# Products of halves one block earlier, weight additions on Pool, and finer steps in a retention and FFN kernel

## The chip, the cores and the metric

The kernel runs on one core of a Trainium2 chip. The metric is device time in microseconds, the median of several runs of one program. The kernel before had 993.59 us (992.89 to 993.91 in 3 runs).

## The reference

All is float32. x has 4 sequences of 1024 tokens and 512 features, here 4096 rows.

```
xn  = layernorm(x)
q, v = xn @ Wq.T, xn @ Wv.T                 # 16 heads of 32
ret[t] = lam * ret[t-1] + v[t]              # per sequence and head
y   = layernorm(q * ret) * silu(xn @ Wg.T)
x1  = x + layernorm(y @ Wo.T)
n   = layernorm(x1)                         # weights below rounded to float8 e4m3
h   = silu(n @ gate_w * gate_s) * (n @ up_w * up_s)      # 512 -> 1536
out = x1 + layernorm(h @ down_w * down_s)
```

## The kernel before, in words

The rows are cut into 8 blocks of 512 tokens, numbered 0 to 7. For each block there is an attention part (class `Retention`: xn, v with its scan, q, y, g, the output projection o and x1) and an FFN part (class `Ffn`: gate, up, fuse, down). Block 0's attention stands alone at the start. Then the loop at L973 runs over t = 0 to 7; in each turn the FFN of block t, in 12 iterations i (128 of the 1536 inner features each), is woven together with the attention of block t+1 (`b`), the preparation of block t+2 (`n`: statistics, xn, its transpose by way of DRAM) and the end of the FFN of block t-1 (`l`: scale, statistics, residual).

Every instruction goes through `InOrder` (L66): an engine executes its instructions in the order in which the program text emits them. Nothing overtakes on an engine's queue, nor on the queues from which SP issues DMAs. Engines wait for one another by semaphores that the tile framework places.

TensorE's work for a block is: v, q and g, 4 projections each of 4 float32 matmuls of 512 columns (L282); o, 4 more; a mean and a variance over features by a matmul with a constant matrix, whose input is split into a rounded upper half and a rest (`halves`, L575); and the FFN, in which gate, up and down are each 8 matmuls of a cheaper type (fp32r), 4 for the upper half of x1n and 4 for its rest.

From block FAST on (L330, 3 before) v, q and g are computed from 7 products of halves instead of 8: the 512 by 512 weight is cut into four quarters, and so is the input; `order` (L333) lists the products, `product` (L461) does one, 4 matmuls of 256 columns, and adds it up with the others on DVE. Four of the seven need sums of weight quarters (5, 6, 7 and 3 in `weight_sums`, L339); these were made on DVE in the first two iterations of t = 1 and stored to DRAM. The weights of the products are fetched into a ring of 4 buffers by SP (`fetch_weights`, L364), which takes the place of the square weights in SBUF. Four of the seven need differences of input quarters (`input_sums`, L445), which Pool computes into `t_sums` from the transposed xn. Products 1, 6 and 2 of v are done in the last iteration of the turn before.

Three other things lie around the change:

- Rounding of the FFN weights to float8 values (`round_weights`, L183) goes on piece by piece during block 0's attention and the first 8 iterations of t = 0: for each piece an integer mask on DVE (the "unit"), two activations on ACT, an addition and a subtraction on DVE, 1024 elements a row, and then the load of a further piece on SP. `rounds(3)` does one piece.
- A search for weights that overflow (`find_over`, L228) runs over the FFN weights on ACT in t = 1 in 24 activations, spread by the list `look`; `pass_over` (L247) adds up what it found in t = 2 with a matmul, and puts it into the down scale.
- PSUM has 2 banks for attention (`pa0`, `pa1`), 2 for gate and up (`pf`), 4 for down.

Of the kernel before, what the change touches and what calls it, by code (L numbers as in the profile page):

```python
# [10 lines left out]
F32 = mybir.dt.float32  # L11
# [4 lines left out]
ALU = mybir.AluOpType  # L16

P = 128
# [5 lines left out]
def retention_ffn_sandwich(  # L24
# [20 lines left out]
    NT, D = x.shape  # L45
# [20 lines left out]
    class InOrder:  # L66
# [113 lines left out]
    def load_piece(n):  # L180
        sp.dma_start(as_dst(parts[places[n][0]], n), pieces[n][1])
# [64 lines left out]

    def pass_over():  # L247

        dve.reduce_sum(total, over, mybir.AxisListType.X)
        po = ps_tile("over_all")  # L250
        pe.matmul(po[:, :1], mean_w, total, start=True, stop=True)
        dve.tensor_scalar(total, po[:, :1], 3e38, 3e38, ALU.mult, ALU.mult)
        dve.tensor_scalar(total, total, 0.0, None, ALU.mult)
        dve.tensor_scalar(ds_sb, ds_sb, total, None, ALU.add)


    def stats(src, mv):
# [78 lines left out]
    squares = {"v": (wvT, wv_sb), "q": (wqT, wq_sb), "g": (wgT, lambda: wg_sb)}  # L336
    operands = {}

    def weight_sums():  # L339

        for k, (src, w) in squares.items():
            w = w() if callable(w) else w
            v = src.rearrange("(c p) f -> p c f", p=P)
            a11, a12, a21, a22 = (w[:, i : i + 2, o : o + H] for o in (0, H) for i in (0, 2))
            operands[k] = {1: v[:, 0:2, 0:H], 2: v[:, 2:4, 0:H], 4: v[:, 2:4, H:D]}
            done = {}
            for j, x, y, op in (
                (5, a21, a22, ALU.add), (6, 5, a11, ALU.subtract),
                (7, a11, a21, ALU.subtract), (3, a12, 6, ALU.subtract),
            ):  # L350
                t = work.tile([P, D], F32, tag="tok", name=f"sum_{k}{j}", bufs=4)
                done[j] = t.rearrange("p (c f) -> p c f", c=2)
                x, y = (done[o] if isinstance(o, int) else o for o in (x, y))
# [5 lines left out]
    sums = weight_sums()  # L359
    RING = 4  # L360
    total_products = len(order) * (NB - FAST)
    fetched = [0]
# [476 lines left out]
    for n in range(4):  # L839
        load_piece(n)  # L840
    wg_sb = load_square(wgT, "wg_sb")
    a = Retention(0, x_first)
    a.new_xnT()
    warm(14)
# [18 lines left out]
    b = Retention(1)  # L863
# [108 lines left out]
    l = None  # L972
    for t in range(NB):  # L973
        f, n = Ffn(a), None
        fast = b is not None and b.fast
        for i in range(NI):
            if t > 0 and (t > 1 or i):
                (f if i else l).rest((i - 1) % NI)
            if t == 0 and i == 0:
                n = Retention(2)  # L980
# [10 lines left out]
            if l and b and not fast and i == 3:  # L991
                l.norm(0)
                l.add(0)
                l.norm(1)
                l.add(1)
# [8 lines left out]
            if n and i == 6 and t > 0:  # L1004
                n.stats(2)
                n.stats(3)
                n.rstd()
                if n.fast:
                    n.shift()
            if b and not fast and i == 5:  # L1010
                b.z(0)
            if b and i >= 8:
# [21 lines left out]
            if b and not fast and t > 0 and i < 3:  # L1034
                b.v(i + 1)
                b.scan(i + 1)
            if l and b and not fast and i == 2:
                l.stats(0)
                l.stats(1)
            if b and not fast and i == 3:  # L1040
                b.halves()
                units()
                if t == 0:
                    rounds(3, now=False)
                b.g_of(0)
                b.mean()
                b.center_y()
                if t == 0:
                    n.stats(3)
                    n.rstd()  # L1050
                    n.shift()
            if b and not fast and i == 4:
                b.halves()
                if t == 0:
                    rounds(3, now=False)
                b.g_of(1)
                b.var()
            if b and not fast and i == 5:
# [2 lines left out]
            if b and not fast and i == 6:  # L1061
                b.g_of(3)
                b.z(2)
                if t == 0:
                    b.z(3)
            if b and 7 <= i <= 10:
                b.o(i - 7)
            if b and i == 8:
# [14 lines left out]
            if b and not fast and i == 4:  # L1083
                b.rstd_y()
            if n and i == 11:
                if n.fast:
                    n.products(2)
                else:
                    n.v(0)
                    n.scan(0)  # L1090
# [28 lines left out]
            for _ in range((look[i] + 1) // 2 if t == 1 else 0):  # L1119
                next(search)  # L1120

            if l and b and not fast and i == 2:
                l.stats(2)
                l.stats(3)
                l.rstd()
# [5 lines left out]
            if l and b and not fast and i == 3:  # L1131
                l.norm(2)
                l.add(2)
                l.norm(3)
                l.add(3)
            if b and not fast and t > 0 and i < 3:
                b.q(i + 1)
                b.y_of(i + 1)
            if b and not fast and i == 6 and t > 0:
                b.z(3)  # L1140
            if n and i == 5 and t == 1:
                n.stats(0)
                n.stats(1)
            if n and i == 6:
                n.new_xnT()
            if b and 7 <= i <= 10:
# [1 line left out]
            if b and i >= 9:  # L1148
                b.rest_of(i - 9)
            if n and t > 0 and 6 <= i <= 9:  # L1150
                n.norm_x(i - 6, n.fast)
                n.send_x(i - 6)
            if t == 0 and i in (5, 6):
                n.send_x(2 * i - 10)
# [3 lines left out]
            if b and n and i == 11:  # L1158
                b.rest_of(3)
            if n and i == 11:  # L1160
                if n.fast:
                    n.product()
                    n.input_sums(3, 4)
                else:
                    n.q(0)
                    n.y_of(0)

            if i == f.lag:
                f.sums()
# [21 lines left out]
            if n and n.fast and i == 11:  # L1191
                n.product()
            if n and t > 1 and i == 5:
# [19 lines left out]
        l, a, b = f, b, n  # L1213
# [68 lines left out]
```

## Time and profile before

| | before |
|---|---|
| median of 3 runs | 993.59 us |
| the profiled execution | 991.89 us |
| its span, first to last instruction | 990.1 us |
| granted TensorE clock | 0.998 |
| busy PE / DVE / ACT / POOL | 968.6 / 657.1 / 365.3 / 256.4 us |
| one f32 projection, 4 matmuls of 512 columns | 3.43 us |
| one FFN group, 8 fp32r matmuls of 512 columns | 1.83 us |
| block 2's first v matmul to block 3's | 192.27 to 315.39 us |
| one turn with a fast block, from t = 3 on | 118.6 us |

A line of a timeline has the start in us from the span's start, the duration, the engine, the line of the code (here always L74, the recording helper), the operation, out<-in by the program's tile names, the shape, and how many instructions are merged; in brackets the idle time before it and who ended it. A line of waits has who waited for whom, the us in total, how often, and the longest. Names: pv, pq, pg are projections or products of v, q, g; pfg, pfu, pd those of the FFN; po the output projection; mu and var the mean and variance; half a half of their input; mv the layernorm statistics; scr the weights that are rounded; seen the search; xnT the transposed xn.

### The profile page before, as it was taken

Reading aid. Unit: us, or ns where it says so; the run is one execution under the profiler, and the core shown is the slowest. Engines: PE = TensorE matmul, PEld = TensorE weight load, DVE = VectorE, ACT = ScalarE, POOL = GpSimd, SP = SyncE. Lnnn points to the kernel's source line nnn. Section 1 sums busy time; section 2 is a strip of 40 time slices with the busy share of each in tenths; the row PEclk is TensorE's granted clock in tenths of the full one; section 3 lists DMA queues with packets and bytes.
Section 4 is the critical chain, followed back from the end, with each engine's and each line's share of the span. In section 5 each row is a group of like instructions: output and inputs, shape, how many; then the busy total and the mean of one; then the engine's idle time right before and its main releaser. Section 6 shows DMA issues by size and latency. Waiting matters only on the chain.

```text
span 990.1 us, 11037 instructions
## 1 busy us (share of the span) xinstructions
PE 968.6 (98%) x3878; PEld 722.0 (73%) x3878; DVE 657.1 (66%) x1006; ACT 365.3 (37%) x549; POOL 256.4 (26%) x337
## 2 busy tenths in 40 slices
PE   9999999999999999999999999999999999999996
PEld 7455766666666878678876788767887788877885
DVE  5996978548746567665686566866567656756445
ACT  3556575433765125221432114321152211512223
POOL 1405121203314033240513305132141312322020
PEclk9999999999999999999999999999999999999999
DMA  9312314412136326253243633245241542213021
GB/s 295 119 64 73 119 64 104 130 64 85 65 98 149 126 69 229 80 144 118 85 128 90 160 91 109 94 129 157 76 149 57 136 138 75 75 32 117 0 86 43
DMA packets 85223, 104.56 MB, mean 106 GB/s; under 512 B 7728, under 2 KB 49712, under 8 KB 85168
## 3 DMA queue, kind: packets, MB, share of 16 engines
q1 hardware_dynamic: 83584, 102.92, 34.5%
q10 hardware_dynamic: 1584, 0.94, 0.5%
q8 instruction: 31, 0.51, 0.2%
q14 instruction: 24, 0.20, 0.1%
HBM read 71.06 MB, written 32.77 MB: 105 GB/s over the span
## 4 chain that ended last, share of the span: by engine, by line
PE 86%; DVE 6%; POOL 3%; ACT 2%; issue 1%; DMA 1%; ACTq 0%; DVEq 0%; SPq 0%; POOLq 0%
PE pfu L74 16%; PE pfg L74 16%; PE pd L74 15%; PE pv L74 10%; PE pg L74 10%; PE pq L74 9%; PE po L74 9%; POOL t_sums L74 1%; DVE st L74 1%; DVE fuse L74 1%; POOL mv L74 1%; DVE scr L74 1%; ACT seen L74 1%; POOL x L74 1%; DVE d L74 1%
## 5 line engine op out<-in xcount | busy, mean ns | idle before, releaser
L74 PE MATMUL pfu<-x1nT,up_sb 128*128 128x512 f32 x768 | 212.1, 418 | 0.0
L74 PE MATMUL pfg<-x1nT,gate_sb 128*128 128x512 f32 x768 | 194.3, 395 | 0.4 <-DVE x1nT L74 0.4
L74 PE MATMUL pd<-down_sb,fuse 128*128 128x512 f32 x720 | 187.2, 401 | 0.0
L74 PEld LDWEIGHTS pfu<-x1nT,up_sb 128*128 128x128 f32 x768 | 144.5, 188 | 44.4 <-issue 14.4
L74 PEld LDWEIGHTS pfg<-x1nT,gate_sb 128*128 128x128 f32 x768 | 144.1, 188 | 30.4 <-DVE x1nT L74 0.8
L74 PEld LDWEIGHTS pd<-down_sb,fuse 128*128 128x128 f32 x720 | 135.3, 188 | 29.3 <-issue 1.7
L74 ACT CAST fuse<-gate 128x512 fp32r<-128x512 f32 x90 | 55.7, 618 | 236.4 <-DVE gate L74 236.4
L74 ACT ACTIVATE gate<-pfg,gs_sb 128x512 f32<-128x512 f32 x96 | 65.7, 684 | 206.2 <-PE pfg L74 206.1
L74 DVE SCALAR_TENSOR_TENSOR gate<-pfu,us_sb,gate 128x512 f32<-128x512 f32 x96 | 71.6, 746 | 82.8 <-PE pfu L74 82.8
L74 PE MATMUL po<-wo_sb,y 128*128 128x512 f32 x256 | 114.5, 592 | 0.0
L74 POOL TENSOR_SCALAR mv<-mv 128x1 f32<-128x1 f32 (+1 forms) x82 | 18.6, 226 | 302.6 <-DVE mv L74 301.6
L74 PEld LDWEIGHTS po<-wo_sb,y 128*128 128x128 f32 x256 | 48.2, 189 | 50.3 <-issue 46.9
L74 DVE TENSOR_TENSOR fuse<-gate,fuse 128x512 fp32r<-128x512 f32 x90 | 75.6, 840 | 9.1 <-ACT fuse L74 9.1
L74 POOL TENSOR_TENSOR ysum<-y 128x256 f32<-128x256 f32 (+1 forms) x13 | 13.5, 1038 | 188.8 <-DVE y L74 161.1
L74 POOL TENSOR_TENSOR x<-x,x1n 128x512 f32<-128x512 f32 x32 | 46.7, 1460 | 45.7 <-DVE x1n L74 36.7
L74 DVE BATCH_NORM_STATS2 st<-x 128x6 f32<-128x512 f32 x64 | 43.6, 681 | 13.7 <-POOL x L74 11.2
L74 DVE TENSOR_TENSOR mids<-pv,mids 128x512 f32<-128x512 f32 x25 | 17.3, 691 | 46.3 <-PE pv L74 43.4
L74 POOL TENSOR_TENSOR mv<-mv,nhalf 128x1 f32<-128x1 f32 (+1 forms) x75 | 45.3, 604 | 6.2
L74 PE MATMUL pv<-xnT,wv_sb 128*128 128x512 f32 (+1 forms) x120 | 42.9, 508 | 1.6 <-ACT xnT L74 1.6
L74 PE MATMUL pv<-t_sums,w_ring 128*128 128x256 f32 x160 | 38.3, 382 | 5.6 <-POOL t_sums L74 5.6
L74 PE MATMUL pq<-xnT,wq_sb 128*128 128x512 f32 (+1 forms) x112 | 43.4, 531 | 0.0
L74 PE MATMUL pg<-xnT,wg_sb 128*128 128x512 f32 x96 | 43.0, 592 | 0.0
(156 smaller groups left out, 1334.5 us busy)
## 6 DMA issues: line engine op xcount, KB each, us to landing
kept<-x SPq DMA_DIRECT2D x32, 256.0 KB, 2.1
x<-kept SPq DMA_DIRECT2D x32, 256.0 KB, 3.7
x<-in_x SPq DMA_DIRECT2D x28, 256.0 KB, 4.1
out<-d SPq DMA_DIRECT2D x27, 256.0 KB, 2.0
xnT<-mx SPq DMA_DIRECT2D x24, 256.0 KB, 4.8
mxs<-xs SPq DMA_DIRECT2D x84, 64.0 KB, 1.8
x1n<-mxs SPq DMA_DIRECT2D x21, 256.0 KB, 2.7
mx<-xn SPq DMA_DIRECT2D x20, 256.0 KB, 2.3
```

Of the source, the lines that this page charges most:

```text
L74: return lambda *args, **kwargs: tc.keep_in_program_order(op(*args, **kwargs))
```

## The change

- FAST is 2: block 2, too, goes by products of halves. Block 1 is the last that goes the old way, so the branches for slow blocks in later turns fall away.
- The weights' sums are made on Pool, in iterations 0 to 2 of t = 0 (v, then q, then g, 4 additions each), into 4 buffers used in turn; SP stores them at the end of the same iteration. The ring of weights is set up at the end of iteration 7 of t = 0, not of iteration 6 of t = 1.
- The first of Pool's four input additions is emitted at the end of iteration 10, not in iteration 11; the second stays in iteration 11.
- The search's last step is a generator in three parts: the sum at the end of iteration 0 of t = 2, the matmul in iteration 1 before the up product, the rest behind the gate step of iteration 1. It was all at the end of iteration 1.

```diff
     def pass_over():
         dve.reduce_sum(total, over, mybir.AxisListType.X)
+        yield
         po = ps_tile("over_all")
         pe.matmul(po[:, :1], mean_w, total, start=True, stop=True)
+        yield
         dve.tensor_scalar(total, po[:, :1], 3e38, 3e38, ALU.mult, ALU.mult)
         dve.tensor_scalar(total, total, 0.0, None, ALU.mult)
         dve.tensor_scalar(ds_sb, ds_sb, total, None, ALU.add)
+        yield
...
-    FAST = 3
+    FAST = 2
...
-                dve.tensor_tensor(done[j], x, y, op)
-                operands[k][j] = dram.tile([P, 2, H], F32, tag=f"sum_{k}{j}", name=f"dsum_{k}{j}", bufs=1)
-                sp.dma_start(operands[k][j], done[j])
-                yield
+            pool.tensor_tensor(done[j], x, y, op)
+        return done
+
+    def keep_sums(k, done):
+        for j, t in done.items():
+            operands[k][j] = dram.tile([P, 2, H], F32, tag=f"sum_{k}{j}", name=f"dsum_{k}{j}", bufs=1)
+            sp.dma_start(operands[k][j], t)
...
+            if t == 2 and i == 1:
+                next(passing)
...
+            if t == 0 and i < 3:
+                k = "vqg"[i]
+                done = weight_sums(k)
...
-            if n and n.fast and i == 11:
-                n.input_sums(1, 2)
+            if n and i == 11:
+                n.input_sums(2)
             units()
             f.up(i)
             f.fuse(i)
...
+            if t == 2 and i == 1:
+                next(passing)
             if fast and i < 6:
                 b.product()
...
+            if n and i == 10:
+                n.input_sums(1)
+            if n and i == 11:
                 n.product()
+            if t == 0 and i < 3:
+                keep_sums(k, done)
...
-            if t == 1 and i < 2:
-                for _ in range(6):
-                    next(sums, None)
-            if t == 1 and i == 6:
+            if t == 0 and i == 7:
                 t_sums = wpool.tile([P, 4, 2, H], F32, tag="wv_sb", name="t_sums")
...
-            if t == 2 and i == 1:
-                pass_over()
+            if t == 2 and i == 0:
+                next(passing)
```

More of the change, by code (lines that the diff above doesn't have):

```diff
@@ L254, in pass_over @@
         dve.tensor_scalar(ds_sb, ds_sb, total, None, ALU.add)
+        yield
+    passing = pass_over()
     def stats(src, mv):
@@ L335, in retention_ffn_sandwich, with weight_sums @@
     banks = {"v": {1: 0, 6: 1, 5: 0}, "q": {1: 1, 6: 0, 5: 1}, "g": {1: 0, 6: 0, 5: 1}}
-    squares = {"v": (wvT, wv_sb), "q": (wqT, wq_sb), "g": (wgT, lambda: wg_sb)}
+    squares = {"v": (wvT, wv_sb), "q": (wqT, wq_sb)}
     operands = {}
[L339 to L353, printed above, removed]
-                dve.tensor_tensor(done[j], x, y, op)
-                operands[k][j] = dram.tile([P, 2, H], F32, tag=f"sum_{k}{j}", name=f"dsum_{k}{j}", bufs=1)
-                sp.dma_start(operands[k][j], done[j])
-                yield
-    sums = weight_sums()
+    def weight_sums(k):
+        src, w = squares[k]
+        v = src.rearrange("(c p) f -> p c f", p=P)
+        a11, a12, a21, a22 = (w[:, i : i + 2, o : o + H] for o in (0, H) for i in (0, 2))
+        operands[k] = {1: v[:, 0:2, 0:H], 2: v[:, 2:4, 0:H], 4: v[:, 2:4, H:D]}
+        done = {}
+        for j, x, y, op in (
+            (5, a21, a22, ALU.add), (6, 5, a11, ALU.subtract),
+            (7, a11, a21, ALU.subtract), (3, a12, 6, ALU.subtract),
+        ):
+            t = work.tile([P, D], F32, tag="tok", name=f"sum_{k}{j}", bufs=4)
+            done[j] = t.rearrange("p (c f) -> p c f", c=2)
+            x, y = (done[o] if isinstance(o, int) else o for o in (x, y))
+            pool.tensor_tensor(done[j], x, y, op)
[4 more added lines that the diff above has]
+            sp.dma_start(operands[k][j], t)
     RING = 4
@@ L841, in retention_ffn_sandwich @@
     wg_sb = load_square(wgT, "wg_sb")
+    squares["g"] = wgT, wg_sb
     a = Retention(0, x_first)
@@ L990, in retention_ffn_sandwich @@
                     l.scale(s)
[L991 to L995, printed above, removed]
             if l and not b and i in (6, 7):
@@ L1007, in retention_ffn_sandwich @@
                 n.rstd()
-                if n.fast:
-                    n.shift()
+                n.shift()
             if b and not fast and i == 5:
@@ L1033, in retention_ffn_sandwich @@
                 b.y_of(i + 2)
[L1034 to L1039, printed above, removed]
+            if t == 0 and i < 3:
+                k = "vqg"[i]
+                done = weight_sums(k)
             if b and not fast and i == 3:
@@ L1042, in retention_ffn_sandwich @@
                 units()
-                if t == 0:
-                    rounds(3, now=False)
+                rounds(3, now=False)
                 b.g_of(0)
@@ L1047, in retention_ffn_sandwich @@
                 b.center_y()
[L1048 to L1051, printed above, removed]
+                n.stats(3)
+                n.rstd()
+                n.shift()
             if b and not fast and i == 4:
                 b.halves()
-                if t == 0:
-                    rounds(3, now=False)
+                rounds(3, now=False)
                 b.g_of(1)
@@ L1063, in retention_ffn_sandwich @@
                 b.z(2)
-                if t == 0:
-                    b.z(3)
+                b.z(3)
             if b and 7 <= i <= 10:
@@ L1082, in retention_ffn_sandwich @@
             f.fuse(i)
-            if b and not fast and i == 4:
+            if t == 0 and i == 4:
                 b.rstd_y()
             if n and i == 11:
[L1086 to L1090, printed above, removed]
+                n.products(2)
                 b.turn_x1n(3, "pf")
                 b.upper_of(3)
+            if t == 2 and i == 1:
+                next(passing)
             if fast and i < 6:
@@ L1120, in retention_ffn_sandwich @@
                 next(search)
[L1122 to L1125, printed above, removed]
             if l and not b and i in (4, 5):
@@ L1130, in retention_ffn_sandwich @@
                     l.rstd()
[L1131 to L1143, printed above, removed]
             if n and i == 6:
@@ L1150, in retention_ffn_sandwich @@
             if n and t > 0 and 6 <= i <= 9:
-                n.norm_x(i - 6, n.fast)
+                n.norm_x(i - 6, True)
                 n.send_x(i - 6)
@@ L1160, in retention_ffn_sandwich @@
             if n and i == 11:
[L1161 to L1166, printed above, removed]
+                n.product()
+                n.input_sums(3, 4)
             if i == f.lag:
@@ L1190, in retention_ffn_sandwich @@
                 b.rstd_y()
-            if n and n.fast and i == 11:
+            if n and i == 10:
+                n.input_sums(1)
+            if n and i == 11:
                 n.product()
-            if n and t > 1 and i == 5:
+            if t == 0 and i < 3:
+                keep_sums(k, done)
+            if n and t > 0 and i == 5:
                 n.stats(0)
                 n.stats(1)
-            if t == 1 and i < 2:
-                for _ in range(6):
-                    next(sums, None)
-            if t == 1 and i == 6:
+            if t == 0 and i == 7:
                 t_sums = wpool.tile([P, 4, 2, H], F32, tag="wv_sb", name="t_sums")
```

## The prediction

> **What bounds the kernel now.** The page first: the TensorE matmul row is busy for 98% of the span, and the chain that ended last is 86% PE.
>
> ```profile
> span 990.1 us, 11037 instructions
> PE 968.6 (98%) x3878; PEld 722.0 (73%) x3878; DVE 657.1 (66%) x1006; ACT 365.3 (37%) x549; POOL 256.4 (26%) x337
> PE 86%; DVE 6%; POOL 3%; ACT 2%; issue 1%; DMA 1%; ACTq 0%; DVEq 0%; SPq 0%; POOLq 0%
> ```
>
> So an edit counts for what it takes from PE's row, and for each moment at which PE must stand still. Next, the waits of PE, all that there are above 0.9 us:
>
> ```profile
> PE pv L74 <- POOL t_sums L74: 5.6, 5, 1.1
> PE pv L74 <- ACT xnT L74: 1.6, 2, 1.2
> PE var L74 <- ACT half L74: 1.4, 1, 1.4
> PE pv L74 <- DMA mxs<-xs: 1.3, 1, 1.3
> PE idle L74 <- DVE nhalf L74: 1.0, 1, 1.0
> PE over_all L74 <- DVE total L74: 1.0, 1, 1.0
> ```
>
> Three of them are the change's: t_sums (x's additions, once per fast block), over_all (the search's last step), and the DMA, which is block 3's x arriving. Last, the timeline of DVE where PE leaves block 0's third up product and comes to block 1's mean:
>
> ```profile
> 117.54 0.68 DVE L74 TENSOR_TENSOR fuse<-gate,fuse 128x512 fp32r<-128x512 f32 x1
> 118.14 0.68 DVE L74 BATCH_NORM_STATS2 st<-x 128x6 f32<-128x512 f32 x1
> 118.86 0.18 DVE L74 BATCH_NORM_AGGREGATE mv<-st 128x2 f32<-128x6 f32 x1
> 118.96 0.66 DVE L74 TENSOR_TENSOR half<-ysum,half 128x512 fp32r<-128x512 f32 x1
> ```
>
> The second half of the mean's matmul needs that "half", which ends at 119.62; PE's mean is at 118.83 to 120.01. DVE has no idle time from 108.81 to there. In this place DVE, not PE, sets the pace, with nothing to spare.
>
> **What the Trainium skill says.** GPSIMD Engine Reference, 1. Specifications: Pool's SBUF interfaces are shared with VectorE, and it collides with DVE instructions that have two SBUF inputs or run in a two-port mode. VectorE: DVE Perf Modes, The perf-mode tier table: a float32 tensor_tensor runs at 1x, a tensor_scalar from SBUF at 2x, an operand in PSUM excludes the two-port mode. The trace agrees on both. Its timelines of DVE and of Pool in block 0's attention:
>
> ```profile
> 45.30 1.98 DVE L74 TENSOR_TENSOR scr<-scr 128x1024 f32<-128x1024 f32 x1
> 47.31 2.18 DVE L74 TENSOR_TENSOR gate_sb<-scr 128x1024 fp32r<-128x1024 f32 x1
> 49.42 1.76 DVE L74 TENSOR_SCALAR scr<-scr 128x1024 int32<-128x1024 int32 x1
> ```
> ```profile
> 44.93 5.70 POOL L74 TENSOR_TENSOR sqsum<-sqsum,sq 128x512 f32<-128x512 f32 x3 [1.29 <-ACT sq L74]
> ```
>
> Alone these take 1.22, 1.22 and 0.68 us on DVE, and 1.26 each on Pool. Here they alternate: each waits for the other's to end, so DVE stood 0.76, 0.96 and 1.08 us, about 1 us for each Pool instruction. Operations with PSUM (gate, y from pq) and bn_stats show no such wait beside a busy Pool. ScalarE activation tables: per-element evaluation and per-set limits, What a function is on this engine: changing between table sets costs 1283 ns; the trace has 1.28 us.
>
> **The change, part by part.** The sum is against the profiled execution: 990.1 us of span and 1.8 around it, 991.89; the median shown is 993.59, 1.7 above, and the difference is put on that.
>
> 1. *Block 2's products.* Twelve projections of 3.43 us (chain, "PE pv L74 x8") become 21 products of about 1.73 (three iterations with three products each, 322.82 to 333.49, are 10.67 us, less six FFN groups of 1.82 make 5.2 per three): 41.2 against 36.4, less 4.8. Checked on whole blocks: block 2's first product to block 3's is 192.27 to 315.39, less its 1.34 wait, 121.8; a fast block 435.63 to 554.22, less its 1.12 wait, 117.5. That says 4.3, which I take. **-4.3** (bounds 4.0 to 5.0).
>
> 2. *The weights' additions on Pool.* Twelve Pool instructions, 1.26 us each, in block 0's first three iterations, behind ysum (101.53 to 102.82). Taking twelve DVE additions out of block 1 (0.68 us each) gains nothing: PE waits for no DVE there. But on Pool they meet DVE's weight rounding, which is saturated. I walk the two engines' orders with the alternation rule, DVE's own durations from its row in the trace and Pool's 1.26 (number = end in us; what has to alternate is in capitals, and each such step starts 0.1 before the other's end):
>
> ```
> Pool YSUM 102.8 | DVE UNIT 103.4 | V5 104.5 | ROUND 105.6 | V6 106.7 | ROUND 107.8
> V7 108.9 | FUSE0 109.5 | V3 110.6 | DVE statistics 110.2, y 110.8, gate1 111.5
> Pool YSUM 112.2 | UNIT 112.8 | Q5 113.9 | ROUND 115.0 | Q6 116.1 | ROUND 117.2
> Q7 118.3 | FUSE1 118.9 | Q3 120.0 | statistics 119.6, gate2 120.3 | G5 121.3
> UNIT 121.9 | G6 123.0 | ROUND 124.1 | G7 125.2 | ROUND 126.3 | G3 127.4
> FUSE2 128.0 | statistics 128.7 | HALF starts 128.7
> ```
>
> Each q and g addition needs its buffer's store landed (issued on SP 0.4 us apart, 2 us to land): in time. Gate1 frees the PSUM bank that PE needs at 110.36, so PE stands 1.2 there; behind it are the down products and all else. "Half" starts at 128.7, not 118.96, and PE's mean is late by 9.7, the 1.2 included. In short: twelve collisions at 0.9, less 1 us of DVE idle used up at 107.8. After it everything at mean, centring and variance follows as before, shifted. **+9.7**. Below: if a third of the collisions fall on DVE's statistics or PSUM work, 7. Above: 1.08 each with no idle used, 12. A gain is excluded, as PE waits for DVE here now already. Stores: SP's weight loads stand behind four stores each, but each load waits for DVE's rounding longer than Pool takes; nothing.
>
> 3. *x's additions sooner.* In steady blocks Pool's two additions run 435.92 to 438.58, and PE, free at 437.36, starts its second product at 438.64. Now the first addition is issued one iteration earlier. But it needs the transposed x: the last of its four loads is issued at 429.0 and lands 5.9 later, 434.9. It ends at 436.2; the statistics' pair for the last x1 tile (0.19 and 0.55, now at 435.13) stands behind it, ends at 436.95, then the second addition, 438.2. Gain about 0.35 a block, not 1.1, four blocks: **-1.4** (0 to -4.5, if the load lands 1 us sooner). Block 3's x lands at 315.2 already late: first addition to 316.5, the pair, second to 318.6 against 318.4: **+0.1**. Block 2 has such a wait for the first time: Pool's add ends at 191.4, addition to 192.7, pair to 193.5, second to 194.8; PE is ready for it at 193.8: **+1.0** (0.5 to 1.1).
>
> 4. *Block 2 fast beside the search.* ACT's 24 search activations (1.57 us each, and 0.19 to read the sum) stay in block 1's FFN, now amid the fast block's ACT work. Most fit: ACT idles 2 to 6 us in front of each gate. One doesn't. In iteration 4 a search step takes a buffer that the variance's matmul reads, so ACT waits for that matmul, then searches 1.57, then loads a table (1.28, hidden under the wait in a steady block), and only then takes the root. On the steady block's clock: root end 502.2 instead of 499.8; reciprocal to 505.6; DVE catches up by two idle gaps of 0.22 and 0.91; the last gated y is 1.15 late. The output projection starts at 516.86 with next to no slack, so PE stands **+1.0** (0 to 3).
>
> 5. *The search's end in parts.* Its 0.96 wait goes. But the matmul now sits in front of the second up product, and its result is read by DVE only behind that product's gate step (0.67), while PE's next half product needs the same bank: PE waits about 1.1 there. Blocks cost 120.16 with the step and 118.60 without; Behind it on PE stands the rest of the iteration. With 0.2 for the matmul that is 1.3 against 1.56: **-0.2** (-1.0 to +0.5).
>
> 6. *Early ring loads.* Four loads of 256 KB enter SP's queue ahead of block 1's transposes at 168. They may delay ACT by 2 us at 178; the next PE need, a PSUM bank at 190.3, is met at 187.4 now. **0** (to +1).
>
> Sum: -4.3 + 9.7 - 1.4 + 0.1 + 1.0 + 1.0 - 0.2 = **+5.9 us**. 991.89 + 5.9 = 997.8 in a profiled execution; 993.59 + 5.9 = 999.5 for the median.
>
> **The rivals.** *The collisions hide* (faster). Mechanism: Pool's twelve additions fit between DVE's rounding instructions instead of alternating with them. It decides once a Pool addition costs DVE under 0.32 us (3.8 of other gain over twelve); at none the time is 989.8. For: the sums depend on one another, so Pool leaves gaps. Against: all three cases at 45 to 51 us alternate, as does the 2.31 us rounding step at 97.22 beside ysum. Chance 0.15. *Half of it* (the same): stores land late, Pool's additions for g slip behind the mean's half, where DVE's idle 2.87 us at 126 takes part of the loss; 4.9 instead of 9.7 gives 994.7. Chance 0.12. *More waits*: on top of the forecast, the search in iterations 5 and 6 or the ring loads cost 3 to 4 us: 1003. Chance 0.08. That the additions sooner do little is in the forecast already.
>
> **How the numbers follow.** Forecast 0.65 (own range 996.5 to 1002.5). A measurement can tell about 0.2%, 2 us, from no change. Faster by more: 0.15; within: 0.12; slower: 0.73. The range of 8 in 10 reaches from the faster case's near side to the case of more waits, 989.5 to 1003.5.
>
> **What would show it.** Right: Pool's twelve sums lie between 102.8 and about 128, its instructions longer than 1.26, DVE's rounding steps stretched to about 2.2; PE waits for DVE "half" at block 1's mean by about 8 us; t_sums waits of about 0.8 remain in the later blocks; a wait of about 1 us for y at block 2's first output projection; a wait of about 1 us after over_all. Wrong: the mean within 3 us of its present place, or t_sums waits gone.

## The result and the profile after

The changed kernel has 1003.19 us (1001.9 to 1003.75, 4 runs), the kernel before 993.24 us (992.22 to 993.91, 4 runs): ratio 1.0099, 95% interval 1.0082 to 1.0117, slower. The forecast was 999.5. A ratio here and below is to executions of the kernel before that were timed along with the run in question, so that equal medians can have slightly different ratios. The profiled execution has 1001.9 us, its span is 1000.1; before it was 991.89 and 990.1, so 10.0 us have to be found. In the lines PE is TensorE, DVE VectorE, ACT ScalarE and POOL GpSimd.

The page of the kernel after, the lines that answer to those of before:

```profile
span 1000.1 us, 11277 instructions
PE 968.1 (97%) x3950; PEld 737.0 (74%) x3950; DVE 662.3 (66%) x1007; ACT 369.9 (37%) x556; POOL 283.9 (28%) x358
PE 74%; DVE 10%; DMA 5%; ACT 4%; POOL 4%; issue 2%; SPq 1%; ACTq 0%; DVEq 0%; POOLq 0%
```

PE is busy for the same time as before (968.6), in a longer span, although block 2's work shrank by some 4 us: part of what remains ran slower, as shown below. The rest of what was added is standing time, and on the chain that ended last PE's share fell from 86% to 74%. Where PE stands, in the waits of the kernel after:

```profile
PE pv L74 <- POOL t_sums L74: 8.9, 6, 2.8
PE mu L74 <- DVE half L74: 5.9, 1, 5.9
...
PE pv L74 <- DMA xnT<-mx: 1.5, 1, 1.5
PE po L74 <- DVE y L74: 1.2, 1, 1.2
PE pfu L74 <- DVE gate L74: 1.1, 1, 1.1
...
PE pq L74 <- DVE total L74: 1.0, 1, 1.0
```

New are mu (5.9), pfu (1.1) and po (1.2), and t_sums grew from 5.6 to 8.9; over_all's 1.0 has become pq's. The wait of 1.4 at the variance is gone only because PE itself comes there later.

The largest part lies where it was forecast. VectorE from block 0's first gate step to block 1's "half", in the timeline of the kernel after (before, "half" started at 118.96):

```profile
103.43 2.29 DVE L74 TENSOR_TENSOR scr<-scr 128x1024 f32<-128x1024 f32 x1
...
107.85 1.78 DVE L74 TENSOR_TENSOR fuse<-gate,fuse 128x512 fp32r<-128x512 f32 x1
109.56 0.68 DVE L74 BATCH_NORM_STATS2 st<-x 128x6 f32<-128x512 f32 x1
...
122.09 2.18 DVE L74 TENSOR_TENSOR down_sb<-scr 128x1024 fp32r<-128x1024 f32 x1
...
126.67 0.93 DVE L74 TENSOR_TENSOR half<-ysum,half 128x512 fp32r<-128x512 f32 x1
```

And GpSimd in the same stretch:

```profile
102.91 1.73 POOL L74 TENSOR_TENSOR sum_v<-wv_sb 128x512 f32<-128x512 f32 x1
104.71 2.14 POOL L74 TENSOR_TENSOR sum_v<-sum_v,wv_sb 128x512 f32<-128x512 f32 x1
...
112.88 2.35 POOL L74 TENSOR_TENSOR sum_q<-wq_sb 128x512 f32<-128x512 f32 x1 [0.49 <-DMA dsum_v<-sum_v]
...
119.10 1.27 POOL L74 TENSOR_TENSOR sum_q<-wq_sb,sum_q 128x512 f32<-128x512 f32 x1
```

The two alternate: four of the six rounding steps of 1.22 take 2.2 or 2.3, the fuse step of 0.68 takes 1.78, and eleven of GpSimd's twelve additions of 1.26 take 1.7 to 2.35. The statistics (0.68) beside them are not stretched, and one addition, at 119.10, took 1.27. "Half" starts 7.7 later than before. PE, first in the kernel before and then in the kernel after:

```profile
120.01 2.00 PE L74 MATMUL pfu<-x1nT,up_sb 128*128 128x512 f32 x8
121.85 1.98 PE L74 MATMUL pd<-down_sb,fuse 128*128 128x512 f32 x8
123.67 1.98 PE L74 MATMUL pfg<-x1nT,gate_sb 128*128 128x512 f32 x8
...
131.51 2.00 PE L74 MATMUL pfu<-x1nT,up_sb 128*128 128x512 f32 x8
```
```profile
127.66 0.80 PE L74 MATMUL mu<-half,mean_r 128*128 128x512 f32 x1 [5.88 <-DVE half L74]
128.25 3.62 PE L74 MATMUL pfu<-x1nT,up_sb 128*128 128x512 f32 x8
131.66 2.80 PE L74 MATMUL pd<-down_sb,fuse 128*128 128x512 f32 x8
134.30 1.98 PE L74 MATMUL pfg<-x1nT,gate_sb 128*128 128x512 f32 x8
...
140.57 2.02 PE L74 MATMUL pfu<-x1nT,up_sb 128*128 128x512 f32 x8
```

The up product behind the mean starts 8.24 later; that is the additions, with 0.1 of a later start. Then the up and down products take 3.62 and 2.80 instead of 2.00 and 1.98, and the gate product is 10.63 late: 2.4 us go without any wait. The granted TensorE clock was 0.57 from 127.66 to 134.30; in the kernel before it was 1.00 from 120.01 to 123.67. Of the 10.63, 1.57 come back, since PE no longer waits at the variance, and PE's first product behind the variance moves from 131.51 to 140.57: 9.06 in all. Followed along PE: 9.35 at block 2's first product (192.11, now 201.46), 9.39 at block 3's first (315.39, now 324.78), 9.78 at block 3's second, 10.0 at the end. So block 2's whole turn, which was to bring 4.3, brings nothing. Its work shrank as forecast: 123.28 less 1.34 of waiting before, 123.32 less 2.81, 1.15 and 1.50 after, that is 121.94 and 117.86, a gain of 4.1. The waits took all of it back.

### The profile page after: what moved, and what is told of

Its sections match the earlier page's. It is cut to its first block, busy times and chain, and to the rows that moved or that the text cites. A ratio compares the mean times of both kernels' runs of the same rounds, so it can differ in the third digit from the quotient of the medians.

```text
span 1000.1 us, 11277 instructions
## 1 busy us (share of the span) xinstructions
PE 968.1 (97%) x3950; PEld 737.0 (74%) x3950; DVE 662.3 (66%) x1007; ACT 369.9 (37%) x556; POOL 283.9 (28%) x358
## 4 chain that ended last, share of the span: by engine, by line
PE 74%; DVE 10%; DMA 5%; ACT 4%; POOL 4%; issue 2%; SPq 1%; ACTq 0%; DVEq 0%; POOLq 0%
PE pfu L74 13%; PE pfg L74 13%; PE pd L74 13%; PE pv L74 9%; PE pq L74 9%; PE pg L74 8%; PE po L74 6%; DMA xnT<-mx 3%; DVE scr L74 2%; POOL t_sums L74 2%; DVE st L74 1%; DVE fuse L74 1%; POOL mv L74 1%; DVE gate L74 1%; ACT seen L74 1%
## 5 line engine op out<-in xcount | busy, mean ns | idle before, releaser
L74 DVE TENSOR_TENSOR fuse<-gate,fuse 128x512 fp32r<-128x512 f32 x90 | 78.6, 873 | 11.3 <-ACT fuse L74 11.3
L74 PE MATMUL pv<-t_sums,w_ring 128*128 128x256 f32 x192 | 45.9, 382 | 8.9 <-POOL t_sums L74 8.9
L74 DVE TENSOR_TENSOR mids<-pv,mids 128x512 f32<-128x512 f32 x30 | 20.7, 692 | 49.7 <-PE pv L74 43.5
L74 PEld LDWEIGHTS pv<-t_sums,w_ring 128*128 128x128 f32 x192 | 35.9, 189 | 16.5 <-POOL t_sums L74 11.3
L74 PE MATMUL pq<-t_sums,w_ring 128*128 128x256 f32 x192 | 45.4, 379 | 1.0 <-DVE total L74 1.0
L74 PE MATMUL pg<-t_sums,w_ring 128*128 128x256 f32 x192 | 45.7, 381 | 0.0
```

What stands on the lines that cost most here:

```text
L74: return lambda *args, **kwargs: tc.keep_in_program_order(op(*args, **kwargs))
```

## The experiments

The theory: (a) the additions are in the wrong place, beside a saturated VectorE that PE waits for; (b) block 2's gain is eaten by queue places, the ring's loads ahead of block 1's transposes and the search step ahead of the root. The rivals: the additions would cost as much on VectorE or elsewhere; the waits belong to a fast block 2 itself.

**Without the additions.**

```diff
-            t = work.tile([P, D], F32, tag="tok", name=f"sum_{k}{j}", bufs=4)
-            done[j] = t.rearrange("p (c f) -> p c f", c=2)
-            x, y = (done[o] if isinstance(o, int) else o for o in (x, y))
-            pool.tensor_tensor(done[j], x, y, op)
+            done[j] = a21 if isinstance(x, int) else x
```

> Leaves out the twelve additions of weight quarters (the stores to DRAM stay, with unsummed quarters, so the products are not the reference's). My theory, that the additions on Pool and DVE's weight rounding take turns at SBUF in block 0's FFN: PE's mean of block 1 comes back to about 119 us, the waits for half (5.9) and gate (1.1) and the stretched rounding steps go, and the time falls by 9 us, to about 994. Rival, that the twelve stores on SP's queue or their DMA traffic hold up the weight loads and so the rounding: the stores are still there, so the time stays within 2 us of 1003.

Measured: 993.88 us, ratio 1.0015 (1.0008 to 1.0023). The waits at mu and pfu are gone, the rounding steps take 1.21 and 1.23 again, and the variance's 1.4 is back. Against the ratio of the changed kernel, 1.0099, the additions cost 8.3 us. But even a kernel that need not add anything is not faster than before: t_sums 8.0, po 1.2 are still there. So (a) is most of the loss, and the missing gain is another matter.

**The additions on VectorE, same place.**

```diff
-            pool.tensor_tensor(done[j], x, y, op)
+            dve.tensor_tensor(done[j], x, y, op)
```

> The same twelve additions at the same places, on DVE instead of Pool. My theory, that the cost is the waiting of the two engines for one another: on DVE an addition takes 0.60 us of the queue and nothing waits, 12 x 0.6 = 7.2 less about 1 us of idle, so the mean is late by about 6 instead of 9, and the time is about 1000. Rival, that Pool relieves DVE at least in part: moving the work back to DVE makes it slower than 1003, by up to 7 us.

Measured: 1008.13 us, ratio 1.0156 (1.0139 to 1.0173), a miss. VectorE's timeline of this kernel says why:

```profile
113.13 0.69 DVE L74 TENSOR_TENSOR sum_q<-wq_sb 128x512 f32<-128x512 f32 x1 [2.83 <-DMA dsum_v<-sum_v]
...
124.37 0.69 DVE L74 TENSOR_TENSOR sum_g<-wg_sb 128x512 f32<-128x512 f32 x1 [3.49 <-DMA dsum_q<-sum_q]
...
132.05 0.66 DVE L74 TENSOR_TENSOR half<-ysum,half 128x512 fp32r<-128x512 f32 x1
```

The four buffers come free only when the stores have landed. On GpSimd that wait cost 0.49 and 0.80; on VectorE all else queues behind it, 2.83 and 3.49. PE then waits 6.29 for a gate step and 2.71 for "half", and the up products behind these two waits take 3.5 each instead of 2.0. Without these 6.3 us, "half" would start at 125.7, an estimate from these lines, one microsecond before the changed kernel's: an addition on GpSimd takes from VectorE about what it would take there (0.69). A kernel with only the additions on VectorE, without the waits for stores, was not run.

**The ring of weights later.**

```diff
-            if t == 0 and i == 7:
+            if t == 0 and i == 9:
                 t_sums = wpool.tile(...)
```

> The ring of weights is set up, and its first four loads issued, at the end of iteration 9 of block 0's FFN instead of 7. Theory: the four loads stood ahead of block 1's transposes on SP's queue and on the DMA engines, which made ACT and then Pool's x addition late and PE's first wait for t_sums 2.8 us instead of 1.0; the time falls by 1.8, to about 1001.4, and that wait is about 1.0. Rival, that the wait is Pool's own order (addition, statistics, addition): the wait stays 2.8 and the time 1003.

Measured: 998.84 us, ratio 1.0066 (1.0051 to 1.0082), by the ratios 3.3 better than the changed kernel. First the changed kernel, SP's queue and then ScalarE:

```profile
177.11 0.49 SPq L74 DMA_DIRECT2D w_ring<-in_wvT  x1
...
178.63 0.47 SPq L74 DMA_DIRECT2D w_ring<-dsum_v  x1
179.20 4.01 SPq L74 DMA_DIRECT2D mxs<-xs  x4
```
```profile
190.45 0.62 ACT L74 CAST x1nT<-x1n 128x512 fp32r<-128x512 f32 x1 [3.96 <-DMA x1n<-mxs]
```

Four loads of the ring stand in front of the transposed x1; ScalarE stands 3.96 for it, with the next x1n behind; GpSimd's addition of x waits for that x1n, and the differences of inputs stand behind that addition. With the late ring ScalarE's wait is 0.76, and PE's first wait for t_sums 0.86 instead of 2.81. These 2.0 are shown; the other 1.3 I can't place (the profiled execution, 3.6 better, started 0.8 earlier).

**x's differences together in iteration 11 again.**

```diff
-                n.input_sums(2)
+                n.input_sums(1, 2)
...
-            if n and i == 10:
-                n.input_sums(1)
```

> Both of x's first two additions in iteration 11 again, as before the change, all else as after it. My theory, that the earlier addition is held up by the load of the transposed x and then holds up the statistics: the later blocks' t_sums waits stay at about 1.1 us, the first one grows by 0.8, and the time is 1003 to 1004. Rival, that the earlier addition does save its 1.26 us wherever it is used: six waits grow by about 1, the time is about 1009.

Measured: 1003.18 us, ratio 1.0113 (1.0098 to 1.0128). In the trace only the first wait for t_sums grows, from 2.8 to 3.9; those of the later blocks do not. By the trace the earlier addition is worth 1.1 us once, and nothing in the steady blocks; in the times the two kernels can't be told apart.

**The search step away from the root.**

```diff
-    look = [2, 2, 2, 0, 1, 3, 3, 3, 2, 2, 2, 2]
+    look = [3, 2, 2, 0, 0, 3, 3, 3, 2, 2, 2, 2]
```

> The changed kernel with one of block 1's search activations moved from the middle of iteration 4 (between the variance's matmul and the root) to the end of iteration 0, where ScalarE idles 4 us. My theory (the wait of 1.15 us at block 2's first output projection is the search step in front of the root): that wait goes, the root's activation follows the variance's matmul without a search in front of it, nothing else moves; total 1.1 less than the changed kernel, ratio to before 1.0088. Rival (the wait is the fast block's own, as its softer start meets the search of iterations 5 and 6): the wait stays above 0.8 us and the time is the changed kernel's.

Measured: 1001.99 us, ratio 1.009 (1.0065 to 1.0115). ScalarE behind the half of block 2's variance, first in the changed kernel, then here:

```profile
262.32 0.63 ACT L74 CAST half<-sqsum 128x512 fp32r<-128x512 f32 x1
266.40 1.58 ACT L74 ACTIVATE seen<-gate_sb,neg_max 128x1536 fp8e4<-128x1536 f32 x1 [3.46 <-PE var L74]
...
269.39 0.69 ACT L74 ACTIVATE rstd<-var,eps_sb 128x512 f32<-128x512 f32 x1
```
```profile
264.45 0.62 ACT L74 CAST half<-sqsum 128x512 fp32r<-128x512 f32 x1
...
268.75 0.69 ACT L74 ACTIVATE rstd<-var,eps_sb 128x512 f32<-128x512 f32 x1 [2.38 <-PE var L74]
```

From half to root it is 7.07 with the search step and 4.30 without, and PE's wait of 1.15 at the output projection is gone from the waits. The cause of the wait is shown; the microsecond itself is within the interval of the time.

**The search's end whole again.**

```diff
-            if t == 2 and i == 1:
-                next(passing)
...
-            if t == 2 and i == 1:
-                next(passing)
...
-            if t == 2 and i == 0:
-                next(passing)
+            if t == 2 and i == 1:
+                for _ in passing:
+                    pass
```

> The changed kernel with the search's last step whole again, at the end of iteration 1 of block 2's FFN, as in the kernel before. My theory (the wait only changed its place): the wait of 0.98 us of the q product for VectorE's total goes, a wait of about 0.96 us of the matmul over_all for the sum comes back, and the time is the changed kernel's within 0.5 us, ratio 1.0099 to 1.0104. Rival (parting it is worth its wait): 1 us more, ratio 1.011.

Measured: 1001.59 us, ratio 1.0089 (1.0073 to 1.0105). The wait for over_all is back with 1.0, that of pq is gone. Parting it is worth nothing that can be seen.

**The additions later, in place.** v's four in iteration 4, q's and g's in iterations 7 to 10, one to three at a time; the ring in iteration 9.

```diff
-            if t == 0 and i < 3:
-                k = "vqg"[i]
-                done = weight_sums(k)
...
             if b and i >= 8:
                 b.x1_moments(i - 8)
+            if t == 0:
+                some_sums({8: 2, 9: 2, 10: 1}.get(i, 0))
...
             if b and 7 <= i <= 10:
                 b.o_moments(i - 7)
+            if t == 0:
+                some_sums({4: 4, 7: 1, 8: 1, 9: 1}.get(i, 0))
```

> The changed kernel with the twelve weight additions still on GpSimd, but later in block 0's FFN: v's four in iteration 4, those of q and g one, two or three at a time in iterations 7 to 10, in gaps in which GpSimd waits for layernorm statistics; they are made in place, in the square weights that are no longer needed, and the ring is set up in iteration 9 and the products' partial sums in iteration 10. My theory (the loss is the place, where VectorE is saturated with rounding and the mean waits for it, not the work): the 9 us at block 1's mean go, up to 2 us of collisions stay in iteration 4; with the 3.3 that the late ring alone was worth this is 990.5 to 992.5 us, ratio 0.998 to 1.000. Rival (twelve additions cost VectorE some 9 us wherever they stand before block 2): 998 to 999, ratio 1.0065.

Measured: 997.44 us, ratio 1.0051 (1.0034 to 1.0067): half of the gain expected. By the number alone the rival (1.0065) would stand; the trace decides against it, as VectorE's "half" is in time again. The wait at mu is gone, but the waits of PE have new lines:

```profile
PE pv L74 <- ACT mids L74: 3.1, 1, 3.1
...
PE pv L74 <- issue: 1.8, 1, 1.8
...
PE pfg L74 <- ACT gate L74: 1.0, 1, 1.0
```

Three stores of g's sums now stand on SP ahead of the ring's loads, and the ring ahead of block 1's third transpose; the first weight comes late (1.8), and ScalarE waits 3.37 for the transposed tile and copies block 2's first product behind that (3.1; the last 0.5 of it for a store of g, whose weights give their place to the partial sums). The gate wait is v's four additions beside iteration 4's rounding.

**The same with product 2 ahead of product 6, and the search step moved.**

```diff
-    order = [("v", j) for j in (1, 6, 2, 7, 4, 5, 3)]
+    order = [("v", j) for j in (1, 2, 6, 7, 4, 5, 3)]
...
-    look = [2, 2, 2, 0, 1, 3, 3, 3, 2, 2, 2, 2]
+    look = [3, 2, 2, 0, 0, 3, 3, 3, 2, 2, 2, 2]
...
```

> The kernel with the later sums, and also the search step moved to iteration 0 and the v products in the order 1, 2, 6, 7, 4, 5, 3, so that the second one needs no difference of inputs from GpSimd. My theory: of the 6 waits for t_sums, about 1.1 us each from block 3 on, nearly all go, and the 1.15 at block 2's output projection; 6 to 7.5 us less than the kernel with the later sums alone, 984 us, ratio 0.9915 to 0.9925. Rival (GpSimd's differences are late for the third product as well, because product 2 in front of it takes only 1.75 us and products 6 and 7 follow each other): half of it, 987 us.

Measured: 1021.23 us, ratio 1.0272 (1.0228 to 1.0316), a clear miss. All waits for t_sums are gone, and worse ones stand in their place. PE and then ScalarE in a steady block of this kernel:

```profile
453.06 1.89 PE L74 MATMUL pv<-xnT,w_ring 128*128 128x256 f32 x8
457.97 3.55 PE L74 MATMUL pv<-xnT,w_ring 128*128 128x256 f32 x8 [3.02 <-ACT mids L74]
```
```profile
456.29 0.62 ACT L74 CAST x1nT<-x1n 128x512 fp32r<-128x512 f32 x1 [4.16 <-DMA x1n<-mxs]
...
457.34 0.58 ACT L74 COPY mids<-pv 128x512 f32<-128x512 f32 x1
```

Product 2 adds into product 1's bank, so it must wait for ScalarE's copy of product 1, and that stands behind a cast that waits for a transfer. Product 6 in between hides this: the 1.1 us for t_sums are the smaller of two waits. That is half of the loss: the profiled execution is 23.8 longer than that of the kernel with the later sums, its waits make up 12 of it, and PE's busy time the rest (978.3 against 966.5). Behind its six waits product 2 took 2.65 to 3.78 five times and 1.99 once, and the granted clock of the whole execution was 0.979, not 0.996.

**x's second difference ahead of the statistics' pair: in the kernel before, and with all else spread.** The statistics' pair are two small GpSimd steps (0.19 and 0.55) for the layernorm of the last x1 tile. In the first kernel only the two differences move, the first to the end of iteration 10 and the second ahead of the pair; the other kernel is the changed one with this, v's sums in block 0's attention, q's in iteration 4, g's in 7 and 8, the ring in 9 and the search step moved.

```diff
+            if n and n.fast and i == 11:
+                n.input_sums(2)
             if b and i >= 8:
                 b.x1_moments(i - 8)
...
-            if n and n.fast and i == 11:
-                n.input_sums(1, 2)
...
+            if n and n.fast and i == 10:
+                n.input_sums(1)
```

> The kernel before (three slow blocks, weight additions on VectorE in block 1) with one thing of the change and a step further: the first difference of inputs at the end of iteration 10, the second ahead of the statistics' pair in iteration 11. My theory (behind the load of x the pair of 0.8 us stands between the two differences and PE waits for the second): the 5 waits for t_sums fall from 1.1 to 0.3 or 0.4 us each, and the pair's delay of 1.3 us is hidden, as the last x1 tile is transposed 1.7 us after it is ready: 988.5 us, ratio 0.9960 to 0.9970. Rival (the last x1 tile then is late, and PE waits for its transposes instead): no gain, ratio 1.000.

> The changed kernel with the sums apart from each other: v's four in block 0's attention (about 51 to 56 us, beside a reciprocal on VectorE), q's four in iteration 4 of block 0's FFN, g's four in iterations 7 and 8, stores with them; the ring of weights in iteration 9; the search step moved as before; v's products in their old order; and the second difference of inputs is issued on GpSimd ahead of the statistics' pair of the last x1 tile, not behind it. My theory (the waits of the kernel with later sums, 1.8 us for the first weight and 3.1 for the partial sum's copy, come from g's stores standing in SP's queue around the ring's loads): both go or fall to 1 us together, the 6 waits for t_sums fall by 0.75 each, the wait at block 2's output projection goes: 986 to 989 us, ratio 0.994 to 0.997. Rival (the ring's four loads themselves delay the transposed x1 wherever they stand, so that a wait of 2.5 us for the copy stays): 990 to 992, ratio 0.998 to 1.000.

Measured: 998.8 us, ratio 1.006 (1.0041 to 1.008), and 1004.82 us, ratio 1.0118 (1.0101 to 1.0134). Both missed. The waits of PE in the first:

```profile
PE pv L74 <- ACT mids L74: 5.4, 5, 1.1
PE pt L74 <- DVE x1n L74: 2.6, 5, 0.5
PE pv L74 <- POOL t_sums L74: 1.6, 4, 0.7
```

VectorE's step behind the pair, in the kernel before and then here:

```profile
435.99 1.47 DVE L74 TENSOR_SCALAR x1n<-x,mv 128x512 f32<-128x512 f32 x1 [0.95 <-POOL mv L74]
```
```profile
440.03 1.48 DVE L74 TENSOR_SCALAR x1n<-x,mv 128x512 f32<-128x512 f32 x1 [3.85 <-POOL mv L74]
```

5.6 for t_sums became 1.6, and 8.0 came in its place. The pair is late by 2.9, not by the 1.3 that I took, since both differences in front of it stand behind the load of x. VectorE stands for it with the gate step behind, ScalarE's cast and copy stand behind the gate step. My 1.7 us of slack at the transposes left out that gate step. The waits account for 4 of the 5.9 by which the profiled execution is longer. The second kernel has these waits too, and v's additions beside the rounding of block 0's attention stretch that as well: PE stands 2.8 for VectorE's copy of the transposed x, and 2.7 for the gate behind q's; the gate product behind that wait took 3.68 instead of 1.98.

**Each sum in a gap.** v's first two on GpSimd in iteration 4, its others on VectorE in iteration 5 (idle 2.04 us there), g's in 7 and 8, q's in 8 and 9. The ring takes the place of v's square weights, in iteration 6, ahead of all transposes.

```diff
+            if t == 0 and i == 6:
+                w_ring = wpool.tile([P, RING, 2, H], F32, tag="wv_sb", name="w_ring")
...
+            if t == 0 and i == 9:
+                t_sums = wpool.tile([P, 4, 2, H], F32, tag="wg_sb", name="t_sums")
+                mids = wpool.tile([P, 4, 2, H], F32, tag="wq_sb", name="mids")
```

> The changed kernel with every sum in a gap that the trace of the kernel with later sums shows: v's first two on GpSimd in iteration 4, its other two on VectorE in iteration 5, where VectorE idles 2.04 us for ScalarE's part of the rounding, g's four on GpSimd in iterations 7 and 8, q's four in iterations 8 and 9; the ring of weights takes the place of v's square weights already in iteration 6, so that none of its loads stands among the transposes of block 1; the differences take the place of g's weights and the partial sums that of q's, in iteration 9; the search step in iteration 0 as before; everything else as in the changed kernel. My theory (each of the losses was a place in a queue): of the waits that the kernel with later sums had beyond those before the change, 1.8 for the first weight, 3.1 for the copy, 1.0 for the gate and 1.2 at the output projection go; what stays is 4.3 of gain less about 1 us for the new wait for t_sums and its neighbours: span 987, 989 us, ratio 0.9960 to 0.9975. Rival (block 1's FFN has no room for a fast block's start in front of it, and another wait takes their place): 992 or more, ratio 1.000 or above.

Measured: 995.99 us, ratio 1.0028 (1.0018 to 1.0037). The waits for the first weight, the copy and the output projection are gone as expected, but 2.8 for t_sums at block 2 are back (product 1 no longer late), and the gate's wait is 1.7. This lies in the rival's range (1.000 or above): other waits took the place of those that went.

**No addition beside rounding on GpSimd.** v's sums all on VectorE, one in iteration 1 and three in iteration 5; q's first on VectorE in iteration 9; block 2's first two differences in iteration 10, as its x landed long before. The edit against the kernel with each sum in a gap, in part:

```diff
-                (dve if k == "v" and j in (6, 3) else pool).tensor_tensor(dst, x, y, op)
+                (dve if k == "v" or (k, j) == ("q", 5) else pool).tensor_tensor(dst, x, y, op)
...
+            if t == 0 and i == 10:
+                n.input_sums(1, 2)
```

> The kernel with each sum in its gap, mended in three places that its trace names: none of v's sums is on GpSimd any more, but one on VectorE in iteration 1 (it waits 1.0 us for PE there) and three in iteration 5 (in the 2.04 us in which it waits for ScalarE); q's first sum is on VectorE in iteration 9 (it waits 1.95 us for GpSimd's addition of x there), so that GpSimd has one sum less ahead of an addition of x; and block 2's first two differences of inputs, whose x has long landed, are issued in iteration 10. My theory (the three waits that were left, 1.7 for the gate, 0.5 for the gate step, 2.8 for t_sums, are those queue places): 5 us less than the kernel with each sum in its gap, of which block 3's wait for x takes none: span 988, 991 us, ratio 0.9965 to 0.9985, faster than both kernels. Rival (three sums on VectorE do not fit 2.04 us and the addition in front of the gate step is on PE's path): 993 to 995, ratio 0.9995 to 1.0015.

Measured: 990.59 us, ratio 0.9987 (0.9981 to 0.9994): faster than the kernel before by 1.3 us, a little less than expected, and than the changed kernel by 11. VectorE and then PE of this kernel:

```profile
107.99 0.68 DVE L74 TENSOR_TENSOR wv_sb<-wv_sb 128x512 f32<-128x512 f32 x1
109.06 0.75 DVE L74 SCALAR_TENSOR_TENSOR gate<-pfu,us_sb,gate 128x512 f32<-128x512 f32 x1 [0.39 <-PE pfu L74]
...
146.88 2.14 DVE L74 TENSOR_TENSOR wv_sb<-wv_sb 128x512 f32<-128x512 f32 x3
```
```profile
195.71 1.89 PE L74 MATMUL pv<-t_sums,w_ring 128*128 128x256 f32 x8
...
199.28 1.99 PE L74 MATMUL pv<-xnT,w_ring 128*128 128x256 f32 x8 [0.85 <-ACT mids L74]
```

The sums fill gaps, and block 2's second product waits for nothing; a wait of 0.85 for the copy has come up behind it.

## Why the prediction was right, and where it was wrong

Right in direction and in its largest cause, 3.7 us short in size: the median lies just above the range of the forecast itself (996.5 to 1002.5) and inside that of 8 in 10. By its steps:

1. *Block 2's products*, -4.3: measured -4.1. The 10.67 us in its working are one iteration with three products and three FFN groups, not three iterations and six groups; the 5.2 for three products is right.
2. *Additions on Pool*, +9.7: measured 9.06 to the product behind the variance, 8.3 by leaving them out. The alternation held, but "half" came 2.0 earlier than walked, since some additions also fell beside statistics: 0.64 of delay for each of twelve additions where I took 0.81. Of the 9.06, 0.8 are no collision at all: PE's slower clock behind the wait, 2.4, less 1.6 of waiting at the variance. No term had these, so that the sum came within 0.7 is in part luck.
3. *x's differences*, -1.4 + 0.1 + 1.0: this step failed. Steady blocks gained nothing (four waits of 0.9 to 1.5, 4.5 in all, as before). Against PE's first product the first difference starts 0.85 sooner (444.88 to 445.44; before 435.92 to 435.63), the second ends only 0.10 sooner: the load landed 0.17 later than taken and the pair takes 0.87 with its gaps, not 0.74. Of the 0.35 a block, 1.4 in all, nothing was left. Block 3 lost 0.4. At block 2 it was 2.8 instead of 1.0, for the reason in step 6.
4. *The search beside a fast block*, +1.0: measured 1.15, at the place and by the way named; the search step moved takes it away.
5. *The search's end in parts*, -0.2: the wait moved to the q product, 0.98 for 0.96; undoing it changes nothing.
6. *Early ring loads*, 0: failed. I followed ScalarE's delay of "2 us" to the next PSUM bank only, not to the x1n behind it on ScalarE, GpSimd's addition of x and so to t_sums. ScalarE's wait was 3.96, 3.2 more than with the ring later, and 1.8 to 2 us of this reached PE, where the term had 0.

Measured terms: -4.1 + 9.1 + 0.0 + 0.4 + 2.8 + 1.2 + 0.0 = 9.4 of 10.0; 0.2 more is block 3's wait for x (1.50, was 1.34), the rest is spread. Steps 3 and 6, 1.4 and 1.8, are nearly all by which the terms fell short. Of the rivals, "collisions hide" is refuted by the stretched steps, and "half of it" as well: GpSimd's waits for stores were 0.49 and 0.80. "More waits" (1003), which I gave a chance of 0.08, is nearest to the time: the ring loads cost 1.8 to 2 of the 3 to 4 us that it named. No wait of PE for the search in iterations 5 and 6 shows.

What of (b) is settled: the ring's loads and the search step, when moved, took their waits with them. What stays open is whether a fast block 2 can bring its whole 4.1; the best version brings 1.3.

## What to carry to other kernels

An addition moved from VectorE to GpSimd is not off VectorE while two-input or fast steps on SBUF run there: here an addition delayed VectorE by 0.64, about as much as the addition itself takes there (0.69); look for gaps in which VectorE itself waits. When loads are set earlier in an in-order queue, follow what waits for the transfers behind them through every engine until it reaches the bound one, and not to the first place that holds. A wait of PE can cost more than its length: behind the 5.88 here 2.4 us more went in slower products. A small wait that repeats (1.1 us for t_sums) can hide a larger one: look at what comes second before taking it away.

## What was not expected of the hardware

PE's products ran slower behind some of its waits. After the same wait of 1.37 at block 1's variance, the next up product took 2.00 us in the kernel before and 3.46 in the last kernel. The table by stretch, columns busy us of PE, PE's weight loads, VectorE, ScalarE and GpSimd, then the granted clock; the kernel before and the last one:

```profile
132.00:157.00 25.00, 25.00 (x93) 17.20 (x92) 22.65 (x26) 16.23 (x22) 0.00 (x0) 1.00 0.19 64
```
```profile
132.00:157.00 25.00, 25.00 (x89) 17.68 (x88) 23.71 (x28) 15.34 (x20) 0.00 (x0) 0.93 0.27 92
```

The clock fell to 0.93 in this stretch, and some 1.6 us went with it; the kernel with later sums shows 0.93 there as well, that with each sum in a gap 1.00. The changed kernel lost 2.4 in this way behind its wait of 5.88. A wait does not always bring it: behind 2.81 (changed kernel), 2.78 (each sum in a gap) and 3.12 (later sums) the next product took its usual 1.99. Nor does the program decide alone. The kernel before was timed 71 times along with the experiments: the 22 executions with a mean granted clock of at most 0.996 took 993.5 us on average, the other 49 took 992.1. What sets it off is open.

The gain of the last kernel is not made by this: its executions with at most 0.996 took 991.85 on average and the others 990.47; those of the kernel before, along with it, took 993.19 and 991.76, which is 1.3 more in both groups. A difference of a microsecond or two between two traces should be looked up in the clock before it is given to an edit.
